# New ranks for a list-scheduled eight-layer kernel, and idle TensorE products on the input instead of the identity

## The chip, the cores and the metric

The kernel runs on one core of a Trainium2 chip. The core has five engines that each work through their own queue of instructions in order: TensorE (PE in the profile; its weight loads are PEld), VectorE (DVE), ScalarE (ACT), GpSimd (POOL) and SyncE (SP), which here only issues DMAs. The metric is the time of one execution on the device in microseconds. Runs of one kernel differ somewhat, so a median of several is given, with the lowest and the highest.

## The reference, cut to what matters

The input x has 8 sequences of 256 tokens with 128 channels, all float32. Eight layers follow each other, each as a residual on a layer norm of its input:

```python
x = x + causal_attention(layernorm(x))      # softmax over a lower triangle
x = x + ffn_relu(layernorm(x))              # 128 -> 512 -> 128, with a layer norm of its own at the end
x = x + linear_attention(layernorm(x))      # no softmax
x = x + ffn_relu(layernorm(x))
x = x + retention(layernorm(x))             # 16 heads, decay mask, head norm, silu gate
x = x + ffn_silu(layernorm(x))              # 128 -> 384 -> 128, integer weights scaled by 1/127
x = x + softmax_attention(layernorm(x))     # 16 heads of 8, with low-rank additions to the weights
x = x + ffn_silu(layernorm(x))
```

Within a layer the sequences are independent of each other.

## The kernel before, in words

The 8 sequences are taken in four groups of two, so a group is 512 tokens: four tiles of 128 tokens by 128 channels, kept in x[0] to x[3]. Each group goes through the eight layers in order; the last two are one function, softmax_attention_and_ffn. The four groups are independent, and their work is interleaved on the engines so that one group's products run while another's normalisations, copies and exponentials are under way. Everything goes through 8 PSUM banks, 28 "work" buffers and some smaller pools.

The order of the instructions is not written down. The class Plan is a list scheduler that runs in Python while the kernel is built. Every layer is a generator that yields steps such as "0.86 us on PE" or "give me a bank"; Plan keeps a model clock for each engine, picks for the engine that is free first the step that is able to start and has the smallest key, and lets that generator emit its instructions. The order in which it does so is the order in which they stand in each engine's queue on the chip. The key of a step is the rank of its thread, plus LATE if the step on PE has only just become able to start, and then its age. RANKS holds one rank for each group and layer (a lower rank goes first; the eighth number of a row is that of the last ffn_silu). FIRST and LAST are the ranks of the side jobs: FIRST for the causal weights and for the function pairs_of_scores, LAST for constants, linear_weights, retention_weights, silu_weights and softmax_weights. The last argument of plan.start is the model time before which a job doesn't start. LEEWAY is a model delay between the moment when a score bank has been read and the moment when it counts as free.

The lines that matter below, by the numbers that the profile uses:

- keep_busy (L379) issues products of the identity with itself into a bank that nobody reads. They stand six times at the very start, and four times behind the causal weights' products (L442, L443).
- layernorm: statistics of a tile on VectorE (L511, L512), the reciprocal root on VectorE or GpSimd (L518, L519) and GpSimd (L522, L523), and the scaling on ScalarE (L529) or VectorE (L534), whichever the plan finds free.
- transposed (L549): four transposes of a normalised tile on TensorE, and a copy out of PSUM (L414, on ScalarE or VectorE).
- causal_attention: L587 and L600 value and query products, L622 scores, L627 and L631 mask and maximum on VectorE, L634 exponentials on ScalarE, L641 transposes, L649 to L651 products with the values.
- ffn_relu: L719 (up) and L732 (down). linear_attention: L684 to L696. ffn_silu: L1045, L1051, L1061.
- retention: L855 are the score products (32 rows by 64 columns, 1024 matmuls in the profile), L913 the products within a chunk ("within", 64 by 32, 1024 matmuls), L890, L935 and L943 the rest; L840 masks the scores on VectorE.
- softmax attention: pairs_of_scores issues the score products (L1131) into score banks; VectorE finds maxima of them (L1152) for the first pass, which are transposed (L1165) and sent into l_spread by a DMA (L1173); ScalarE takes exponentials (L1186) in the second pass; L1203 are products with the values, L1216 transposes.
- constants: L430 and L434 fill r_values, l_values, r_spread and l_spread with zeros and ones on ScalarE, once. linear_weights has the product of L457, softmax_weights that of L491.

A float32 product is two passes: it appears in the profile as two weight loads and two matmuls. A transpose is one of each.

## Time and profile before

| | |
|---|---|
| median of 3 runs | 454.65 us (451.44, 454.65, 459.67) |
| the profiled execution | 459.54 us, its span 457.8 us, mean granted clock 0.981 |
| TensorE matmul busy | 436.2 us, 95% |
| VectorE busy | 338.9 us, 74% |
| ScalarE busy | 236.7 us, 52% |
| GpSimd busy | 132.3 us, 29% |
| DMA | 10.90 MB, 24 GB/s mean |

The span runs from the first to the last instruction of the program; the execution's own time has 1.7 us more around it. The profile is one execution, and it lies at the upper end of the runs. In the profile's slices the span is cut into 40 parts of 11.4 us; a digit is the busy share in tenths, PEclk the clock that TensorE was granted. A wait is given as what waited, what it waited for, the sum, how many times, and the longest. "issue" is a wait for which the profile shows no cause. A busy TensorE is not TensorE at its peak: matmuls are pipelined and their ends are modelled.

### The profile page before, as it was taken

The page shows a single profiled execution, that of the slowest core. Times are in us where ns is not written, and L with a number is a line of the kernel's source. Part 1 is how long each engine was busy: PE and PEld are TensorE (multiplying, and loading weights), DVE is VectorE, ACT ScalarE, POOL GpSimd, SP SyncE. Part 2 cuts the span into 40 slices and gives each one's busy share as a digit, 9 for nine tenths or more (in the row PEclk, how much of TensorE's full clock was granted, in tenths as well). Part 3 has the DMA queues.
Part 4 walks back from the last instruction along what each step waited for, and adds up shares of the span by engine and source line. Part 5 has one row for each costly group of instructions (what it writes and reads, how often), then busy time and mean ns, then how long its engine had stood idle before and what let it go on. Part 6 is the DMA issues. An engine that isn't in the chain of part 4 may idle for free.

```text
span 457.8 us, 13125 instructions
## 1 busy us (share of the span) xinstructions
PE 436.2 (95%) x5360; PEld 306.1 (67%) x5360; DVE 338.9 (74%) x979; ACT 236.7 (52%) x497; POOL 132.3 (29%) x239
## 2 busy tenths in 40 slices
PE   7999899999899999989989999989999999999987
PEld 6777687758667675764856556766676665656566
DVE  6698888898689789597958778957697652865143
ACT  3579844653532453413448363477844357264851
POOL 4145658776424541112221120230120021000120
PEclk9999899999999999995989999999999999999999
DMA  7300000003003002500001013000200001100001
GB/s 274 127 0 2 1 1 0 1 13 35 5 18 35 3 3 40 56 2 2 6 3 27 4 35 37 4 5 5 42 9 14 14 26 23 27 2 14 2 2 34
DMA packets 8044, 10.90 MB, mean 24 GB/s; under 512 B 1001, under 2 KB 6889, under 8 KB 7985
## 3 DMA queue, kind: packets, MB, share of 16 engines
q1 hardware_dynamic: 7904, 9.94, 10.0%
q8 instruction: 42, 0.69, 0.6%
q14 instruction: 18, 0.14, 0.1%
q10 hardware_dynamic: 80, 0.13, 0.1%
HBM read 4.56 MB, written 1.05 MB: 12 GB/s over the span
## 4 chain that ended last, share of the span: by engine, by line
PE 74%; DVE 12%; ACT 5%; issue 3%; POOL 2%; DMA 1%; SPq 1%; DVEq 0%
PE bank L1131 17%; PE bank L1203 7%; PE bank L1061 5%; PE bank L1045 5%; PE bank L1051 4%; PE bank L855 4%; PE bank L719 3%; PE bank L732 3%; PE bank L587 3%; PE bank L549 2%; PE bank L890 2%; PE bank L788 2%; PE bank L913 2%; DVE small L511 2%; DVE small L1152 2%
## 5 line engine op out<-in xcount | busy, mean ns | idle before, releaser
L1152 DVE TENSOR_REDUCE small<-bank 128x2 f32<-128x512 f32 x128 | 80.7, 683 | 28.3 <-PE bank L1131 28.1
L1186 ACT ACTIVATE probs<-bank 128x512 f32<-128x512 f32 x128 | 68.1, 598 | 53.0 <-PE bank L1131 50.6
L1131 PE MATMUL bank<-l_spread 32*128 32x256 f32 x1024 | 89.3, 409 | 2.3 <-issue 2.3
L1131 PEld LDWEIGHTS bank<-l_spread 32*128 32x128 f32 x1024 | 56.1, 188 | 26.3 <-issue 12.0
L518 POOL TENSOR_SCALAR small<-small 128x4 f32<-128x4 f32 (+1 forms) x40 | 10.0, 250 | 216.2 <-DVE small L512 201.2
L414 ACT COPY work<-bank 128x512 f32<-128x512 f32 (+3 forms) x86 | 40.2, 484 | 53.5 <-PE bank L549 14.3
L529 ACT ACTIVATE work<-x,small 128x128 f32<-128x128 f32 x80 | 34.7, 485 | 37.8 <-POOL small L523 37.6
L522 POOL TENSOR_TENSOR small<-small,mhalf 128x4 f32<-128x4 f32 (+1 forms) x45 | 43.8, 973 | 6.1 <-DVE small L519 6.1
L511 DVE BATCH_NORM_STATS2 small<-x 128x6 f32<-128x128 f32 x128 | 34.6, 271 | 3.7 <-DMA x<-in_x 3.2
L1203 PE MATMUL bank<-probs,l_values 128*32 128x256 f32 x512 | 34.0, 390 | 0.5 <-DVE work L1225 0.5
L512 DVE BATCH_NORM_AGGREGATE small<-small 128x2 f32<-128x6 f32 x160 | 29.1, 182 | 5.6
L732 PE MATMUL bank<-c_relu,work 128*128 128x128 f32 x256 | 31.9, 277 | 0.0
L719 PE MATMUL bank<-work,c_relu 128*128 128x512 f32 x64 | 30.9, 602 | 0.3 <-DVE work L414 0.3
L732 PEld LDWEIGHTS bank<-c_relu,work 128*128 128x128 f32 x256 | 30.2, 192 | 1.0 <-issue 0.7
L582 DVE TENSOR_TENSOR x<-bank,x 128x256 f32<-128x256 f32 (+1 forms) x36 | 15.9, 448 | 13.2 <-PE bank L587 4.2
L1045 PE MATMUL bank<-work,c_ints 128*128 128x256 f32 (+1 forms) x72 | 24.8, 462 | 0.5 <-ACT work L414 0.5
L1203 PEld LDWEIGHTS bank<-probs,l_values 128*32 128x32 f32 x512 | 13.9, 111 | 16.7 <-issue 6.1
L414 DVE COPY work<-bank 128x512 f32<-128x512 f32 (+3 forms) x26 | 13.7, 535 | 15.2 <-PE bank L1203 6.6
L549 PE MATMUL bank<-ident,work 128*128 128x128 f32 x128 | 23.8, 301 | 0.9 <-ACT work L529 0.7
L1061 PE MATMUL bank<-c_ints,work 128*128 128x128 f32 x192 | 24.6, 279 | 0.1
L1061 PEld LDWEIGHTS bank<-c_ints,work 128*128 128x128 f32 x192 | 22.9, 192 | 2.2 <-issue 1.0
L1051 PE MATMUL bank<-work,c_ints 128*128 128x256 f32 (+1 forms) x72 | 24.0, 456 | 0.0
(151 smaller groups left out, 784.8 us busy)
## 6 DMA issues: line engine op xcount, KB each, us to landing
r_spread<-wide SPq DMA_DIRECT2D x32, 64.0 KB
l_spread<-wide SPq DMA_DIRECT2D x32, 64.0 KB
out<-x SPq DMA_DIRECT2D x8, 128.0 KB
c_retention_qk<-in_retention_qk SPq DMA_DIRECT2D x1, 770.0 KB
x<-in_x SPq DMA_DIRECT2D x3, 256.0 KB
c_retention_vo<-in_retention_vo SPq DMA_DIRECT2D x1, 713.0 KB
c_relu<-in_relu SPq DMA_DIRECT2D x1, 706.0 KB
c_ints<-in_ints SPq DMA_DIRECT2D x1, 576.0 KB
```

The costliest lines, as they stand in the source:

```text
L414: (nc.scalar.copy if e == ACT else nc.vector.tensor_copy)(dst, src)
L511: nc.vector.bn_stats(stats[:, i, :], src[:, i, :])
L522: nc.gpsimd.tensor_tensor(rstd, rstd, minus_half[:, :nt], ALU.pow)
L719: nc.tensor.matmul(ps, w1[:, c * P : (c + 1) * P], yT[:, :N], start=True, stop=True)
L732: nc.tensor.matmul(ps[:, n * D : (n + 1) * D], h[c][:, i * P : (i + 1) * P], w2[:, c, :], start=(c == 0), stop=(c == 3),)
L1045: nc.tensor.matmul(ps[:, :n], w_gate[:, cols], yT[:, :n], start=True, stop=True)
L1051: nc.tensor.matmul(ps[:, :n], w_up[:, cols], yT[:, :n], start=True, stop=True)
L1061: nc.tensor.matmul(ps[:, (i - first) * D : (i - first + 1) * D], h[c][:, i * P : (i + 1) * P], w_down[:, c, :], start=(c == 0), stop=(c == 2),
L1131: nc.tensor.matmul(to[k][:, n * S : (n + 1) * S], seq.spread[rows, j, of_keys, n * P : (n + 1) * P], seq.spread[rows, j, 1 - of_keys, :], ...
L1152: nc.vector.tensor_reduce(nmax[:, h2 % 4 // 2, 2 * (h2 % 2) + k, :], ps[k].rearrange("p (m s) -> p m s", m=2), AX.X, ALU.max, negate=True,)
L1186: nc.scalar.activation(p[:, k, :], ps[k], AF.Exp)
L1203: nc.tensor.matmul(o[32 * i : 32 * (i + 1), (j % 2) * S : (j % 2 + 1) * S], seq.v[:, c, VONE * h : VONE * h + 32], seq.p[h2][0][:, k, c * ...
```

## The change

All 32 ranks, FIRST, LAST and LATE get new numbers, LEEWAY goes from 0.29 to 0.03, and the side jobs get new start times. These change no instruction of their own; they change the order in which Plan emits nearly all of them, and which of ScalarE and VectorE takes a copy or a scaling. The products of keep_busy take the first tile of the input x[0] in both places instead of the identity, and three of them stand at the start instead of six. The first causal attention of group 0 gets three more of them behind its transposes, into a bank of their own; the plan counts 0.21 us for each.

```diff
-LEEWAY = 0.29
+LEEWAY = 0.03
...
 RANKS = [
-    [-0.43, -1.33, -1.23, -2.16, 0.4, -1.26, 1.32, 4.87],
-    [-0.32, 1.61, 0.5, 1.51, -0.96, -0.46, -1.85, 1.67],
-    [2.33, 2.23, 2.97, 7.68, 2.15, -1.02, 3.92, 2.82],
-    [3.09, 3.56, 6.8, 10.82, 2.27, 3.76, -2.79, 2.52],
+    [-4.13, -2.77, -1.79, -1.45, 1.42, 1.01, -0.24, 3.83],
+    [-1.82, 0.93, 5.08, 2.15, 1.79, 4.87, 0.66, 0.66],
+    [-0.37, 1.61, -4.13, 2.32, 5.49, -4.05, 3.4, 4.38],
+    [3.42, 6.69, 6.1, 9.09, 1.61, 0.82, 1.3, 1.92],
 ]
-FIRST, LAST = -3.5, 11.78
-LATE = 1.95
+FIRST, LAST = -4.34, 9.59
+LATE = 1.56
...
-            nc.tensor.matmul(ps[:, :P], ident, ident, start=True, stop=True)
+            nc.tensor.matmul(ps[:, :P], x[0][:, 0, :], x[0][:, 0, :], start=True, stop=True)
 
-    keep_busy(banks[0], 6)
+    keep_busy(banks[0], 3)
...
-    def transposed(y):
+    def transposed(y, waiting=0):
 
         nt = y.shape[1]
         yT = yield get(work)
         ps = yield get(bank)
-        yield step(PE, 0.11 * nt)
+        idle = (yield get(bank)) if waiting else None
+        yield step(PE, 0.11 * nt + 0.21 * waiting)
         for i in range(nt):
             nc.tensor.transpose(ps[:, i * P : (i + 1) * P], y[:, i, :], ident)
+        if waiting:
+            keep_busy(idle, waiting)
+            put(bank, idle)
...
-        yT = yield from transposed(y4)
+        yT = yield from transposed(y4, 3 if parts == 2 else 0)
...
-    plan.start(constants(), LAST, 29.7)
-    plan.start(linear_weights(), LAST, 8.6)
-    plan.start(retention_weights(), LAST, 27.1)
-    plan.start(silu_weights(), LAST, 22)
-    plan.start(softmax_weights(), LAST, 57.7)
+    plan.start(constants(), LAST, 31.1)
+    plan.start(linear_weights(), LAST, 11.9)
+    plan.start(retention_weights(), LAST, 47.5)
+    plan.start(silu_weights(), LAST, 22.5)
+    plan.start(softmax_weights(), LAST, 19)
```

Here parts is 2 only in the causal attention of group 0.

## The prediction

> **What bounds the kernel now.** I read the page first: shares, slices, chain.

> ```profile
> PE 436.2 (95%) x5360; PEld 306.1 (67%) x5360; DVE 338.9 (74%) x979; ACT 236.7 (52%) x497; POOL 132.3 (29%) x239
> ...
> PE   7999899999899999989989999989999999999987
> ...
> PEclk9999899999999999995989999999999999999999
> ...
> PE 74%; DVE 12%; ACT 5%; issue 3%; POOL 2%; DMA 1%; SPq 1%; DVEq 0%
> ```

> TensorE is busy nearly throughout, but the chain is its own for 74% only, and its clock dips in three slices. Next the chain in order of time: where is it not TensorE's?

> ```profile
> 36.62 2.57 PE bank L732 x24
> 39.20 3.78 ACT r_spread L434 x4
> ...
> 46.99 2.82 ACT l_spread L434 x3
> 49.82 0.89 ACT work L634 x4
> 50.70 1.54 ACT work L529 x4
> ```

> From 39 to 53 us it runs through ScalarE, at 60 to 70 through VectorE's statistics (L511, L512). Up to about 160 us TensorE and its feeders share the bound; from there PE rows dominate. Then stretches, cut by me at the clock's steps (columns: length, busy of PE, PEld, DVE, ACT, POOL, clock, DMA share, GB/s):

> ```profile
> 50.10:53.50 3.40, 2.08 (x8) 0.96 (x8) 3.19 (x16) 3.40 (x14) 2.04 (x6) 1.00 0.00 0
> 53.50:56.90 3.40, 3.35 (x13) 2.79 (x14) 1.92 (x10) 2.25 (x6) 2.14 (x5) 0.50 0.01 2
> ...
> 203.70:207.10 3.40, 1.93 (x81) 1.58 (x71) 3.40 (x7) 1.54 (x4) 1.66 (x4) 1.00 0.00 0
> 207.10:210.50 3.40, 3.40 (x18) 1.72 (x10) 3.40 (x8) 0.69 (x2) 1.27 (x1) 0.50 0.01 2
> 210.50:214.00 3.50, 3.50 (x21) 1.96 (x20) 1.74 (x6) 1.39 (x2) 1.52 (x2) 0.50 0.02 5
> 214.00:217.40 3.40, 3.40 (x4) 0.94 (x4) 1.83 (x3) 0.98 (x2) 0.00 (x0) 0.51 0.00 0
> 227.60:231.00 3.40, 1.19 (x120) 1.21 (x98) 1.78 (x4) 1.75 (x4) 1.73 (x3) 1.00 0.02 5
> 231.00:234.40 3.40, 3.36 (x28) 2.08 (x31) 1.39 (x3) 1.08 (x2) 0.00 (x0) 0.50 0.02 5
> ```

> A stretch in which TensorE idles 1.3 to 2.2 of 3.4 us is followed by half clock: for one, three and one such stretches, five in all, each losing 1.7 us of work: 8.5 us. A cold start is hidden from the clock column; the durations of L600 show it (min/median/max ns):

> ```profile
> L600 PE MATMUL bank<-work,a_w x8: 592/595/1061, 12.9 to 31.1; 128*128 128x512 f32 x8
> ```

> 1061 ns at 13 us against 592 later. Last, TensorE's waits:

> ```profile
> PE bank L913 <- issue: 3.8, 2, 2.1
> PE bank L1131 <- issue: 2.3, 1, 2.3
> PE bank L457 <- DMA c_linear<-in_linear: 1.9, 1, 1.9
> PE bank L1165 <- DVE small L1152: 1.6, 2, 1.5
> ```

> The three "issue" waits end at 121.05, 231.04 and 306.40.

> [...] The three waits of about 2 us did not all trip it; only 231 did. [...] The trace has 42 packets and 0.69 MB on its instruction queue. I counted TensorE's instruction list (a float32 product is two loads and two matmuls, a transpose one of each, waits one): the three issue waits fall at counts 1985, 5569 and 7873, each a multiple of 256 less 63. So they are block boundaries. [...] here three cost 6.1 us.

> **The change, step by step.** The sum is made against the profiled execution, 459.54 us (span 457.8), the top of the runs shown; their median 454.65 is 4.9 us, or three half-clock windows, below it.

> 1. Start. Six identity products become three on the input; they must wait for x, which lands at 3.24 (VectorE's first row) instead of starting at 1.42. L442 still starts near 4.5 and the first transposes at 7.3, when VectorE and ScalarE deliver. Three more products (0.43 us each when cold) then fill 8.35 to 9.63, and the product of L457, which waited until 10.28 for its weights, stands behind group 1's transposes. L587 thus starts near 9.6 instead of 11.0: 1.4 us. If real data wake the clock one window sooner, another 1.9 follow: 3.3. Identity products ran from 1.4 to 7.5 without waking it, but no row shows input products. Yet the chain is ScalarE's and VectorE's by 39 us, so an earlier TensorE mostly waits longer. Bounds 0 and -3.3; I take -1.0.

> 2. Idle at 50 to 53.5, 1.86 us, plus one window, 1.7. It ends with the last exponentials L634. In the new order one spread copy of L434 (1.05 us) stands behind them; summing row durations ahead of the last exponential, ScalarE carries 33.2 us for 36.2 and VectorE 49.1 for 51.9. But VectorE's chain at 60 to 70 comes next. Bounds 0 and -3.6; I take -1.0. L491's products move forward by some 37 us of work and wait for the last load; the loads are over by 16 us (DMA share 0.01 from 16.0 to 22.9), so nothing queues behind them.

> 3. Idle at 204.6 to 206.1, 1.47, and its three windows, 5.1. Four maxima (L1152, 2.48 us together) stand between the scores and transpose L1165, covered by one block of L855 alone, 1.16. In the new order twelve products of L1061 stand there: 24 x 0.119 = 2.85, enough. This lies where TensorE is the bound: -6.6. If VectorE's backlog is longer, only the place changes; lower bound of the gain 0.

> 4. The window at 231: -1.7 (bounds 0, -1.7).

> 5. Instruction blocks. In the old order the three waiting blocks hold 1.5 us of work (L913 takes about 12 ns per matmul, 128 in a block) and waited 1.7 to 2.3: a block needs about 3.4 us. Adding row durations block by block and taking what is missing to 3.4 gives 7.1 us before (6.1 seen) and 9.7 after: pairs at blocks 8 and 9 (1.1 + 1.1), 14 and 15 (0.9 + 1.9), 20 (1.6) and 22 (0.4), 30 and 31 (1.8 + 0.8). Those before about 160 us may hide behind VectorE. Bounds +0.7 and +2.6; I take +1.5.

> 6. New half-clock windows at those places: between none and two each, 0 to +13.7; I take one, +1.7, since two of three such waits tripped nothing.

> 7. LEEWAY 0.29 to 0.03: a score bank is handed on 0.26 us earlier in the planner. With row durations laid along each order (queueing at the releasing engine left out), all score products but two before and three after have their bank free over 0.5 us ahead of use: I take 0; bounds 0 and 64 groups x 0.26 = +16.6, the upper end held by no row. The new tail puts 0.7 us of L1061 ahead of its last wait: -0.3 at best, 0 taken.

> Sum: 459.5 - 1.0 - 1.0 - 6.6 - 1.7 + 1.5 + 1.7 = 452.4. Run to run the number of windows varies, so I keep it against the median too: 454.65 holds about two windows, one remains (-1.7), idle 1.47 goes, starts give 2.0, blocks cost 1.5: 451.0. I forecast 451.6, midway.

> **The rivals.** *Everything counts* (chance 0.2): steps 1 and 2 keep their whole gain and no window runs cold: 459.5 - 3.3 - 3.6 - 6.6 - 1.7 + 0.7 = 445.0. For it: PE is busy 95%. Against: the chain at 39 to 70. *Only moved* (0.2): the early gains are absorbed, windows trip as often as in the median run, blocks cost their +1.5: 456. For it: the ranks remove no TensorE work; the product count is the same but for timing. *Crowded blocks* (0.1), the one that ends slower: the paired blocks idle TensorE 2.0 to 2.8 us within 4 us, as long as the 2.2 at 229 which halved the clock. Two windows at each of four places: 459.5 - 6.6 - 1.7 + 2.6 + 13.7 = 467.5. Without early gains it passes the median from one window on, and 463.7 from six.

> **How the numbers follow.** The likeliest case (0.5) gives 451.6, itself 448 to 455. A measurement here tells about 2% from no change: below 445.6 or above 463.7. Faster: half of the first rival and a little of the main case, 0.14; slower: most of the last, 0.08; same: 0.78. The range, from just under the first rival to short of the last: 445 to 460.

> **What would show it.** Right: L587 first near 9.6; L1165 no longer waiting 1.5 us; issue waits at more places than three, in L913; half-clock slices fewer than three. Step 1 is wrong if L600's maximum stays at 1061 ns or the early gain survives to 160 us. The whole is wrong if the issue waits go away or each trips the clock.

## The result, and the profile after

The changed kernel takes 452.68 us in the median of 20 runs (450.76 to 454.24); the kernel before, run beside it on the same chip, takes 456.15 (20 runs, 451.44 to 460.92). The ratio is 0.9942, with a 95% interval of 0.9921 to 0.9963: a small gain, inside the 2% that was forecast as "no change", and 1.1 us from the 451.6 forecast. The ratio leaves out executions that lie more than 1.5% above the fastest of their kernel, so it is nearer to one than the quotient of the medians (0.9924). The profiled execution took 452.34 us, its span 450.5, granted clock 0.991 (before: 459.54, 457.8, 0.981).

In the changed kernel all line numbers beyond the transposes are four higher: L600 has become L604, L913 L917, L1131 L1135, L1165 L1169; the transposes themselves are L550.

The page of the changed kernel, shares, slices of TensorE and of its clock, chain:

```profile
PE 427.5 (95%) x5360; PEld 300.0 (67%) x5360; DVE 345.9 (77%) x992; ACT 245.0 (54%) x492; POOL 133.5 (30%) x239
...
PE   7899899899999998999999999999999999999996
...
PEclk9999899999999998999999999999999999999999
...
PE 72%; DVE 18%; issue 4%; POOL 2%; ACT 2%; DMA 1%; SPq 0%; POOLq 0%; DVEq 0%; ACTq 0%
```

TensorE's busy time fell by 8.7 us although it computes the same: half-clock stretches count as busy (3.40 of 3.40 us from 207.10 on, before), and fewer are left (three windows of 3.4 us make up to 5.1 of it, and the cold start, now shorter, counts as busy too). Busy time is less than the sum of the matmuls, which overlap in the profile: the 1024 of L913, 225 ns each, make 12.9 us of it before. VectorE and ScalarE carry 7 and 8 us more; the plan deals out copies and scalings differently (979 instructions became 992, 497 became 492). The chain's share of ScalarE went from 5% to 2%, that of VectorE from 12% to 18%: the early bound has changed its engine. The chain in order of time (start, length, what) shows where. Before, it ran from 39 to 53 us through ScalarE's copies of L434; now it runs through VectorE, then one normalisation:

```profile
41.84 2.15 DVE work L534 x2
43.99 0.66 DVE work L728
...
46.57 0.52 DVE small L635 x2
47.09 0.60 DVE x L754
...
50.46 1.01 POOL small L522
```

Stretches of the changed kernel, cut at the steps of its clock; the last is the one in which TensorE had waited before (columns as in the prediction: start and end, length, busy of PE, PEld, DVE, ACT, POOL, clock, DMA share, GB/s):

```profile
49.97:53.38 3.41, 2.24 (x11) 1.24 (x12) 3.27 (x16) 3.33 (x9) 1.62 (x5) 1.00 0.01 2
53.38:56.79 3.41, 3.41 (x11) 2.38 (x11) 3.33 (x7) 1.76 (x4) 3.15 (x5) 0.50 0.00 0
169.43:172.84 3.41, 1.34 (x136) 1.18 (x119) 1.61 (x2) 0.59 (x1) 2.14 (x2) 1.00 0.02 5
172.84:176.26 3.42, 3.34 (x14) 1.44 (x14) 1.53 (x3) 0.58 (x1) 0.00 (x0) 0.50 0.00 0
203.70:207.10 3.40, 3.40 (x12) 1.37 (x14) 3.40 (x7) 1.79 (x3) 0.00 (x0) 1.00 0.00 0
```

Two half-clock windows (stretches of 3.4 us at half clock) where there were five. The one at 53 has stayed. The one at 172.84 is new and follows 2.1 us of idle. Between 203.7 and 207.1, where TensorE was idle for 1.47 us and then cold for three windows, it is now busy without a break. One profile does not show all places: in the ten profiles of the new order that this document draws on, a window begins at 52 to 54 us in four, at 90 to 91 in three and at 173 to 176 in eight. The one at 90 follows a wait of 1.82 us for ScalarE's copy L414, ahead of L700, that stands in all ten (the last of the waits below; the kernel before has none there). Among TensorE's waits (what, for what: sum, times, longest) L1169 is no longer near the top, and the waits of which the profile shows no cause lead the list:

```profile
PE bank L917 <- issue: 5.0, 6, 2.1
PE bank L379 <- DMA x<-in_x: 3.3, 1, 3.3
PE bank L700 <- ACT work L414: 1.8, 1, 1.8
```

The cold start no longer reaches the query products (the same line's durations as in the prediction, min/median/max ns):

```profile
L604 PE MATMUL bank<-work,a_w x8: 592/594/595, 10.6 to 33.3; 128*128 128x512 f32 x8
```

To see where the time went I laid the measured row durations along each order and took the difference between a product's start and its place in that sum. This is an estimate, since the places move by some tens of microseconds with the way the rows are weighed. Against the kernel before, the changed one is about 3.2 us ahead after 10 us of work, 1.0 behind after 80, 5.8 behind after 160 (its wait and window at 172 lie there, while the old order was still covered), 2.1 ahead after 210 (the gap of 206 and its windows), 4.4 ahead after 350 and 7.3 at the end.

### The profile page after: what moved, and what is told of

Read it like the earlier page. It is cut to its first block, busy times and chain, and to the rows that moved or that the text cites. A ratio compares the mean times of both kernels' runs of the same rounds, so it can differ in the third digit from the quotient of the medians.

```text
span 450.5 us, 13165 instructions
## 1 busy us (share of the span) xinstructions
PE 427.5 (95%) x5360; PEld 300.0 (67%) x5360; DVE 345.9 (77%) x992; ACT 245.0 (54%) x492; POOL 133.5 (30%) x239
## 3 DMA queue, kind: packets, MB, share of 16 engines
HBM read 4.56 MB, written 1.05 MB: 12 GB/s over the span
## 4 chain that ended last, share of the span: by engine, by line
PE 72%; DVE 18%; issue 4%; POOL 2%; ACT 2%; DMA 1%; SPq 0%; POOLq 0%; DVEq 0%; ACTq 0%
PE bank L1135 16%; PE bank L1207 7%; PE bank L1065 5%; PE bank L1049 5%; PE bank L859 4%; PE bank L736 4%; PE bank L1055 4%; PE bank L723 3%; DVE work L534 3%; DVE small L511 3%; PE bank L917 3%; DVE small L512 2%; PE bank L894 2%; PE bank L591 2%; PE bank L1220 2%
## 5 line engine op out<-in xcount | busy, mean ns | idle before, releaser
L1135 PE MATMUL bank<-l_spread 32*128 32x256 f32 x1024 | 86.5, 401 | 0.0
L518 POOL TENSOR_SCALAR small<-small 128x4 f32<-128x4 f32 (+1 forms) x40 | 11.8, 295 | 242.7 <-DVE small L512 227.2
L414 ACT COPY work<-bank 128x512 f32<-128x512 f32 (+3 forms) x77 | 37.1, 492 | 68.1 <-PE bank L550 27.2
L1135 PEld LDWEIGHTS bank<-l_spread 32*128 32x128 f32 x1024 | 54.5, 184 | 25.7 <-issue 11.3
L529 ACT ACTIVATE work<-x,small 128x128 f32<-128x128 f32 x70 | 30.6, 487 | 26.6 <-POOL small L523 26.5
L511 DVE BATCH_NORM_STATS2 small<-x 128x6 f32<-128x128 f32 x128 | 34.7, 271 | 3.9 <-DMA x<-in_x 3.5
L414 DVE COPY work<-bank 128x256 f32<-128x256 f32 (+3 forms) x35 | 17.9, 521 | 22.8 <-PE bank L1207 12.3
L1207 PE MATMUL bank<-probs,l_values 128*32 128x256 f32 x512 | 33.2, 384 | 1.1 <-DVE work L1057 0.6
L736 PE MATMUL bank<-c_relu,work 128*128 128x128 f32 x256 | 32.4, 278 | 1.2 <-DVE work L728 1.2
L736 PEld LDWEIGHTS bank<-c_relu,work 128*128 128x128 f32 x256 | 30.3, 192 | 4.7 <-issue 2.4
L512 DVE BATCH_NORM_AGGREGATE small<-small 128x2 f32<-128x6 f32 x160 | 29.1, 182 | 5.5
L723 PE MATMUL bank<-work,c_relu 128*128 128x512 f32 x64 | 32.2, 618 | 0.1
L726 ACT ACTIVATE work<-bank,c_relu 128x512 f32<-128x512 f32 x26 | 17.9, 687 | 16.7 <-PE bank L723 15.7
L1049 PE MATMUL bank<-work,c_ints 128*128 128x256 f32 (+1 forms) x72 | 25.3, 463 | 0.7 <-ACT work L414 0.7
L1065 PE MATMUL bank<-c_ints,work 128*128 128x128 f32 x192 | 24.6, 279 | 0.5 <-ACT work L414 0.5
L1051 ACT ACTIVATE work<-bank 128x256 f32<-128x256 f32 (+1 forms) x36 | 15.7, 454 | 16.7 <-PE bank L1049 16.4
L1065 PEld LDWEIGHTS bank<-c_ints,work 128*128 128x128 f32 x192 | 22.9, 192 | 2.7 <-issue 1.1
L1055 PE MATMUL bank<-work,c_ints 128*128 128x256 f32 (+1 forms) x72 | 24.6, 458 | 0.0
```

Of the source, the lines that this page charges most:

```text
L414: (nc.scalar.copy if e == ACT else nc.vector.tensor_copy)(dst, src)
L511: nc.vector.bn_stats(stats[:, i, :], src[:, i, :])
L723: nc.tensor.matmul(ps, w1[:, c * P : (c + 1) * P], yT[:, :N], start=True, stop=True)
L736: nc.tensor.matmul(ps[:, n * D : (n + 1) * D], h[c][:, i * P : (i + 1) * P], w2[:, c, :], start=(c == 0), stop=(c == 3),)
L1049: nc.tensor.matmul(ps[:, :n], w_gate[:, cols], yT[:, :n], start=True, stop=True)
L1055: nc.tensor.matmul(ps[:, :n], w_up[:, cols], yT[:, :n], start=True, stop=True)
```

## The experiments

**Which part does it: the idle products or the order?** Four kernels on one chip, beside 70 runs of the kernel before (457.0 us). The first gives the kernel before the input in its idle products and leaves everything else:

```diff
 # before
-            nc.tensor.matmul(ps[:, :P], ident, ident, start=True, stop=True)
+            nc.tensor.matmul(ps[:, :P], x[0][:, 0, :], x[0][:, 0, :], start=True, stop=True)
```

> The kernel before with x[0] in place of the identity in the ten idle products at the start, order unchanged. Theory (feeders absorb an early TensorE): the clock wakes one or two 3.4 us windows sooner, so the longest L600 falls from 1061 ns towards 592, but VectorE and ScalarE set the pace to about 160 us of the span and the time stays within 0.5 us of before. Rival (idle products carry the gain): about 1.5 to 3 us faster than before. Second rival (data does not matter): L600 stays near 1061 ns and the time at before.

Measured: 457.76 us, ratio 1.0042 (1.0013 to 1.0071). The clock rose at 15.10 us, and the maximum of L600 stayed at 1061 ns, as the second rival had it. The input in place of the identity gains nothing; if anything it costs 0.4%.

The second also moves three of the six products behind the first transposes, as the change does, in the old order:

```diff
 # before, with the edit above
-    keep_busy(banks[0], 6)
+    keep_busy(banks[0], 3)
...
-    def transposed(y):
+    def transposed(y, waiting=0):
...
+        if waiting:
+            keep_busy(banks[1], waiting)
...
-        yT = yield from transposed(y4)
+        yT = yield from transposed(y4, 3 if parts == 2 else 0)
```

> The kernel before with all of the idle products of the change (three on x at the start, four, and three behind the first transposes of group 0, written to a bank that the next products overwrite), old order otherwise. Theory: clock awake near 9 to 12.6 us instead of 16, gain under 1 us at the end of the run (ratio 0.998 to 1.000). Rival (idle products carry the gain): ratio near 0.994, as the whole change.

Measured: 454.78 us, ratio 0.999 (0.9962 to 1.0018). The clock rose at 14.81 us all the same, so the expected 9 to 12.6 was a miss. Its median lies 2.2 us under the kernel before; resampling the 22 and 70 runs gives -3.5 to +0.3 for that difference, so it isn't settled.

The third is the change without any of the idle products' edits: six of the identity at the start, none behind the transposes, new order. (The plan still sets aside their bank and their 0.21 us each, so that the order stays the same.)

```diff
 # changed
-            nc.tensor.matmul(ps[:, :P], x[0][:, 0, :], x[0][:, 0, :], start=True, stop=True)
+            nc.tensor.matmul(ps[:, :P], ident, ident, start=True, stop=True)
...
-    keep_busy(banks[0], 3)
+    keep_busy(banks[0], 6)
...
-            keep_busy(idle, waiting)
```

> The changed kernel's order with the old idle products: six and four on the identity, none behind the first transposes. Theory: the gain lies after 190 us of the span and comes from the order, so the time is that of the changed kernel within 1 us (452.7, ratio 0.992 to 0.996). Rival (idle products carry the gain): at the time of before, 456.

Measured: 452.94 us, ratio 0.9915 (0.9892 to 0.9937): all of the gain. The fourth is the changed kernel with the identity in its idle products (the first hunk above alone):

> The changed kernel with the identity back in its ten idle products, same places. Theory: L604 at 10.6 us of the span takes about 1061 ns per matmul again because the clock wakes at 12.6 or 16 instead of 9, and the time is within 1 us of the changed kernel. Second rival (data does not matter, being busy does): clock awake at 9 as in the changed kernel.

Measured: 452.86 us, ratio 0.9929 (0.9905 to 0.9953). The expectation that the clock then rises only at 12.6 or 16 us was a miss: it rose at 8.03, and in the third kernel at 4.58, when six identity products and the beginning of the causal weights' were all that had run. So products of the identity can wake the clock, and when it wakes makes no difference to the time here. What follows: **the order is the change**. In the new order the idle products add nothing that these runs show (452.94 us without their edits, 452.86 with the identity in all of them); whether they gain something in the old order is the open 2.2 us above.

**Are the waits in L917 the edges of instruction blocks?** A block is put here at 256 instructions of TensorE's list, since the waits stand multiples of 256 apart (1985, 5569 and 7873 in the prediction). The page has 42 packets and 0.69 MB on the instruction queue, 16.4 KB each; TensorE's list has 10,825 instructions in the trace of the kernel before, 258 to a packet. In the traces of both kernels the closest two of these packets start 3.41 us apart (before; 3.45 in the changed kernel), and each of the nine waits over 0.3 us for which no cause is shown ends 1.27 to 1.49 us after one of them has landed. Sixteen tiny products ahead of everything move every block edge by 64 instructions; the order of all else is unchanged.

```diff
 # changed
+    for _ in range(16):
+        nc.tensor.matmul(banks[0][:32, :8], ident[:, :32], ident[:, :8], start=True, stop=True)
     keep_busy(banks[0], 3)
```

> The changed kernel with sixteen tiny products (32 columns by 8 of the identity) put ahead of everything, while TensorE waits for x anyway: 64 more instructions at the head of TensorE's list, the order of all else unchanged. Block theory: the places where TensorE waits for instructions are multiples of 256 in its list, so they fall on other work. Row durations block by block, 3.4 us needed for each: the computed stalls go from 9.7 to 5.4 us. The waits near 218.7 and 226.3 us of the changed kernel and the first one near 298 vanish, the wait of 2.15 near 173 becomes shorter (1.9 at most), and the sum of waits without a shown cause goes from 5.0 to about 3. Time 1 to 3 us below the changed kernel, about 450.5. Rival (the waits belong to the work that stands there, such as the bursts of tiny products, and not to the count): the same waits at the same places and sizes, sum 5.0 again, time 452.7.

Its waits:

```profile
PE bank L919 <- issue: 4.2, 3, 1.9
...
PE bank L861 <- issue: 0.4, 1, 0.4
```

The waits against those computed from row durations, with the prediction's estimate of 3.4 us needed for a block of 256 (us; place in the span):

| changed kernel | computed | measured | shifted by 64 | computed | measured |
|---|---|---|---|---|---|
| 122.0 | 1.07 | 0.49 | 117.9 | 0.95 | 0.38 |
| 125.5 | 1.10 | 0.80 | 125.3 | 1.10 | 1.10 |
| 172.9 | 0.87 + 1.93 | 2.15 | 172.4 | 1.93 | 1.88 |
| 218.7 | 1.63 | 0.43 | - | none | none |
| 226.3 | 0.36 | 0.43 | - | none | none |
| 298.7 | 1.75 + 0.83 | 0.74 | 298.4 | 0.83 | 1.24 |
| all, with those under 0.4 | 9.7 | 5.0 | | 5.3 | 4.6 |

The waits go with the count and not with the work: those at 218.7 and 226.3 are gone, though the same products stand there. Counted in TensorE's list of weight loads, matmuls and waits, those of the changed kernel come after 1985, 2241, 3777, 5057, 5570 and 7873 instructions, those of the shifted one after 1729, 2241, 3777 and 7873: each is a multiple of 256 and 193 more, to within one. So is every wait of this kind over 0.3 us in all fourteen profiles of this document. So the block edges are shown. Their size was computed too large where the shortfall is small or where two short blocks follow each other. The time was 451.83 us (6 runs). Against all 42 runs of the changed kernel, taken in two other rounds, that is 0.9976 (0.9944 to 0.9991 by resampling), 1.1 us, at the low end of the 1 to 3 expected; the sum of waits was to be 3 and is 4.6, a miss.

**Does the gap at 206 cost what step 3 says?** First taken away from the kernel before, by six products in front of the transpose that waited:

```diff
 # before
+        if seq.g == 0 and seq.b == 0 and half == 1:
+            for _ in range(6):
+                nc.tensor.matmul(ps[:, :P], w_lora_o, w_lora_o, start=True, stop=True)
         nc.tensor.transpose(ps[:16, :P], flat_nmax, ident)
...
+            seq.b = b
```

> The kernel before with six products of a constant put right ahead of the one transpose L1165 that waited 1.47 us for VectorE at 206 us, into the bank that the transpose then overwrites; the order is otherwise unchanged. Theory (step 3: the idle stretch halves the clock for up to three windows): the idle there falls from 1.47 to under 0.5 and no half-clock slice follows at 207; the median falls by 1.5 to 3.5 us, since the windows strike in part of the executions only, to about 453.5. Rival (the idle stretch costs only itself, or the windows come elsewhere): the six products cover an idle that VectorE would have caused anyway, no gain, 457. If they come late, the products themselves cost up to 1.4 us.

Measured: 455.39 us against 457.94 beside it, ratio 0.998 (0.9944 to 1.0017). The wait of 1.47 is gone and no window follows at 207, but the interval of the ratio holds both no gain and 2.5 us: inconclusive.

Then added to the changed kernel at a clean place. GpSimd, which is empty there, holds back the fifth L1169 by multiplications by one:

```diff
 # changed; 14 in one kernel, 20 in the other
+        todo["turned"] = todo.get("turned", 0) + 1
+        for _ in range(14 if todo["turned"] == 5 else 0):
+            nc.gpsimd.tensor_scalar(flat_nmax, flat_nmax, 1.0, None, ALU.mult)
         nc.tensor.transpose(ps[:16, :P], flat_nmax, ident)
```

> The changed kernel with fourteen multiplications by one on GpSimd (0.23 to 0.31 us each, on an engine that is empty there from 265 to 280 us) put between the maxima and the fifth transpose L1169, which in the changed kernel starts at 272.99, 2.4 us after the last maximum. TensorE then waits there for 0.9 to 2.0 us, about as long as the stretch of 1.47 us that step 3 priced at 6.6 with three half-clock windows; its order is unchanged, and no profile so far shows a window within 40 us of the place. The runs of the changed kernel had 1.4 half-clock windows on average, those of the kernel before 3.4, each worth 1.2 us by their slope. Theory (an idle stretch of that length halves the clock in a part of the executions, for one window): windows rise to 1.7 to 2.1 on average, the median by 1.5 + 0.6 = 2 us, to about 455. Step 3 as it was priced (three windows each time): 4 or more windows, 458. Rival (it costs only itself or nothing): windows stay at 1.4, 453 to 454.4.

> The same with twenty multiplications: TensorE waits there for 2.3 to 3.9 us. Theory: one window nearly always follows, so 2.2 to 2.5 windows on average and 453 + 3.0 + 1.2 = 457. Step 3 as it was priced: three windows, 460. Rival (windows have nothing to do with this wait): 1.4 windows, 455 to 456.

The multiplications took 0.33 us each, start to start, so the waits came out longer than expected: 2.3 us in place of 0.9 to 2.0, and 4.3 in place of 2.3 to 3.9. With fourteen, the wait, the 3.4 us up to the clock's step, in which it lies, and the 3.4 us after:

```profile
PE bank L1172 <- POOL small L1171: 2.3, 1, 2.3
```

```profile
272.24:275.65 3.41, 1.11 (x18) 0.71 (x11) 2.48 (x4) 0.36 (x2) 2.13 (x9) 1.00 0.00 0
275.65:279.06 3.41, 3.41 (x7) 1.35 (x6) 0.55 (x2) 0.60 (x1) 0.00 (x0) 0.50 0.01 2
```

With twenty, the clock falls while TensorE still waits:

```profile
272.30:275.71 3.41, 0.44 (x9) 0.04 (x4) 2.48 (x4) 0.00 (x0) 2.53 (x11) 1.00 0.00 0
275.71:282.54 6.83, 5.50 (x11) 2.72 (x11) 1.24 (x3) 0.85 (x2) 1.01 (x4) 0.50 0.00 1
```

A wait of 2.3 us brings one half-clock window, one of 4.3 us brings two. Every run lists its mean granted clock, and a window of 3.4 us in some 450 lowers it by 0.0038 (half of 3.4/450), so windows can be counted, to the nearest whole one, in runs without a profile. The last column is the line through each kernel's own runs: its time at no window, and what one more window adds. The slopes are good to about 0.2 (before) and 0.5 (changed), the times at no window to 0.5 and 0.7; the changed kernel's runs have one or two windows only, so its 451.5 lies outside them.

| kernel | runs | median us | windows, mean | us at none + us per window |
|---|---|---|---|---|
| before (four rounds) | 146 | 456.64 | 3.23 | 453.1 + 1.16 |
| changed (two rounds) | 42 | 452.90 | 1.36 | 451.5 + 1.13 |
| changed, wait of 2.3 | 22 | 456.39 | 2.32 | |
| changed, wait of 4.3 | 6 | 459.89 | 3.17 | |

The ratios to the kernel before are 1.002 (1.0 to 1.004) and 1.0102 (1.0054 to 1.0151). The 2.3 us wait adds 3.5 us (452.90 to 456.39) and 0.96 windows: itself and one window. The 4.3 us wait adds 7.0 and 1.8 windows: itself and 2.7. These two kernels and the changed one ran in different rounds; their ratios to the kernel before beside them, set against 0.9942 and 0.9952 for the changed kernel, say the same (3.1 to 3.6 us and 6.9 to 7.3 us more). The theory's medians, 455 and 457, were too low; its waits were shorter than the ones that came out. The rival, that windows have nothing to do with it, falls; so does "three windows each time", for waits of these lengths. A wait of 1.47 us was not added anywhere.

**Why does one wait halve the clock and the next not?** Within each profile, the clock's steps lie whole multiples of 3.413 us apart (in the changed kernel at 9.01, 53.38, 56.79, 172.84 and 176.26: 13, 1, 34 and 1). So within an execution there is a fixed grid of 3.413 us, and where it falls differs from one to the next: after the start of the span, the first edge lies at 2.2 us in the changed kernel, and in the two runs below at 2.8 and 0.1. Cut along this grid, the traces of two runs give a likely reason for a pair that looks alike. The shifted kernel waited 1.88 us at 172.4, within one stretch; with pairing and shift together (below) it waited 1.86 us at 172.0, of which an edge at 170.72 cut off 0.6. First the shifted kernel, then the other, each with the stretch after:

```profile
170.07:173.49 3.42, 1.54 (x85) 1.03 (x68) 1.43 (x3) 1.07 (x2) 1.57 (x1) 1.00 0.00 0
173.49:176.90 3.41, 3.41 (x25) 2.08 (x25) 1.76 (x3) 0.40 (x3) 0.00 (x0) 0.50 0.02 5
...
170.72:174.13 3.41, 2.13 (x46) 1.18 (x46) 1.13 (x3) 0.59 (x1) 0.53 (x1) 1.00 0.02 5
174.13:177.54 3.41, 3.41 (x72) 3.13 (x70) 2.00 (x6) 2.06 (x6) 0.00 (x0) 1.00 0.00 0
```

Over all fourteen profiles, up to 440 us, nine stretches at full clock have TensorE busy for at most 1.34 us, and half clock follows all nine; it follows 16 of the 44 with 1.50 to 2.26 us, and one of the 1688 with more. What decides in the middle group is not shown, nor why half clock lasted three windows after 206 us in the kernel before, with TensorE busy throughout.

**Do lone pairs of score products cost as much as two?** A group of L1135 normally scores two pairs of heads, but near the end some score one. The chain of the changed kernel there:

```profile
380.06 1.06 PE bank L1135 x8
381.12 1.00 PE bank L1207 x16
382.12 1.08 PE bank L1135 x16
```

Eight matmuls hold the path for 1.06 us, sixteen for 1.08. The prediction had no such term. In the trace of the changed kernel 20 of its 74 groups are lone pairs (19 by themselves, as the expectations count them, and one right beside a group of two), in that of the kernel before 22 of 75. The edit lets a second pair join a little earlier:

```diff
 # changed
-                    if sum(i[0] <= plan.now for i in score_bank.items) > 1:
+                    if sum(i[0] <= plan.now + 0.2 for i in score_bank.items) > 1:
```

> The changed kernel with one threshold in pairs_of_scores moved: once only softmax attention is left, a group of score products takes a second pair of heads along when the banks come free within 0.2 us of the model, not only when they are free already. The order is unchanged up to product 2640 of 2828 (about 390 us); behind it 17 groups of a lone pair remain in place of 19, and 54 of two pairs in place of 53. Theory (a lone pair of heads holds TensorE 1.07 us, nearly as long as two pairs with 1.12): 2 x 1.07 - 1.12 = 1.0 us less, 451.6. Rival (the lone groups lie beside waits for banks that the pairing only moves): no difference, 452.7; if pairs then wait for banks, up to 0.5 us slower.

Measured: 451.89 us (9 runs), against the 42 runs of the changed kernel 0.9978 (0.9962 to 0.9994), 1.0 us less, as computed, though the two were not run side by side. So the changed kernel was run again, beside one with this edit and the shift by 64 together:

> The changed kernel once more, unchanged, as the neighbour of the two runs below on the same chip: 452.7 us, 0.99 to 0.996 of the kernel before.

> The changed kernel with both small edits at once: sixteen tiny products at the head (64 more instructions on TensorE's list) and pairs taken along when banks come free within 0.2 us. Theory (the two gains lie in different stretches, waits for instructions at 218 to 298 us and lone pairs after 390 us, and TensorE is the bound in both): 0.8 + 1.0 below the unchanged one beside it, about 451. Rival (each of them was the difference between two chips or two days): within 0.3 us of the unchanged one.

Measured on that chip: 453.35 us for the changed kernel (22 runs, 0.9952 of the kernel before, 0.9932 to 0.9972), 449.75 for both edits (6 runs, 448.57 to 451.81; 0.9898 of the kernel before, 0.9845 to 0.9951). Between the two the ratio of medians is 0.9921 (0.9901 to 0.9951 by resampling): 3.6 us less (2.2 to 4.5), more than the 1.8 expected; where the rest comes from is open. Its windows are 1.17 on average against 1.41, which at 1.2 us each is 0.3 us of it, and its line, through six runs, stands at 448.6 with none. Its profile has no window at all, although the wait at 172 is there with 1.86 us, cut by the grid as above. On this chip this version beats both kernels.

**Is LEEWAY worth nothing?**

```diff
 # changed
-LEEWAY = 0.03
+LEEWAY = 0.29
```

> The changed kernel with LEEWAY back at 0.29, all ranks and start times as in the change; every decision of the plan behind the first score products may come out differently. Step 7's view (LEEWAY moves only banks that are free long before use): 452 to 453 us. Rival (LEEWAY decides, through the test whether banks are free at that moment, how many score groups run with a lone pair, and the ranks fit one LEEWAY only): 25 lone groups stand in the order in place of 19 and the planner's own clock ends 17 us later, so 465 to 470 us, with TensorE idle in new places.

Measured: 471.05 us, ratio to the kernel before 1.0318 (1.0241 to 1.0396), 17.7 us above the changed kernel beside it. 26 lone groups stand in place of 20 (25 and 19 by themselves). From the start of each score product to that of the next instruction on TensorE, the products of L1135 take 92.9 us in place of 81.7, 3.5 of it in waits; that is most of the 13.0 us between the two profiled spans. Why groups of two pairs take longer there was not tried. With the new ranks the old LEEWAY makes a bad plan. This doesn't say what the change's 0.26 us is worth, because the old ranks were made for the old value.

## Why the prediction was right, and where its steps were not

The number was right within 1.1 us and the mechanism of most of the gain was the one named: fewer stretches in which TensorE idles, and so fewer half-clock windows. By the table the gain between all runs of both kernels, 456.64 to 452.90, is 3.7 us: 1.87 windows fewer at 1.16 us make 2.2, and the time at no window fell by 1.6. The forecast was set midway between a sum for one profile (452.4) and one for the median (451.0). By steps:

1. **Start**, -1.0. L591 starts at 9.65, as computed (9.6). The clock rose at 9.01, so the early gain came near the whole bound, 3.2 of 3.3 us, and it was gone by 80 us, absorbed as argued, with VectorE on the chain there; the third kernel, without the edits of the idle products, kept all of the gain. What failed is the reason given: that the input might wake the clock where the identity does not. Why the clock rose at 4.6 to 12 us in every profile of the new order, and at 14.8 to 16.0 in three of four of the old one, is open; the products ahead of it differ too little. In the fourth of the old one it rose at 4.54 and fell again at 11.36, after a wait of 2.47 us for L457's weights.
2. **Idle at 50**, -1.0. Wrong: the stretch before that window still has 1.17 us of idle (1.32 before; the 1.86 of the prediction also counts waits outside it), and the window came. The chain moved from ScalarE to VectorE; the order was still ahead there (L736 starts at 62.08, L732 at 63.40 before), but the lead was gone near 95 us of the span, after the wait of 1.82 us before L700. No step had that wait, nor that it brings a window in three profiles of ten. By the curve the new order is then behind until about 190 us: the sum of the first two steps was -2.0, and the curve shows +5.8 at 160.
3. **Idle at 206**, -6.6. The idle went as the order said: twelve products of L1065 stand ahead of that transpose, now at 214.93, and it starts without a gap. The size was that of one execution: three windows at 1.7 us. The same wait of 1.47 us stands in two more profiles of the old order, with one window after it in one and none in the other, where an edge of the grid cuts it. The added waits show one window for 2.3 us, and the runs put one window at 1.1 to 1.2 us; that it is less than 1.7 because part of it falls where TensorE isn't the bound is likely, but not shown. For the median the price is, as an estimate, 1.5 and up to 1.2.
4. **Window at 231**: gone, worth about 1.2 us by the slope rather than 1.7. The prediction noted that only one of the three waits of about 2 us tripped the clock: along the grid, TensorE was busy for 1.19 us of the 3.41 there, for 1.71 and 1.61 at the other two.
5. **Instruction blocks**, +1.5. Right places, shown by the shift; wrong sizes. 5.0 us (6.1 in a second profile) in place of 9.7, against 6.1 before: the term is about 0 or -1, not +1.5.
6. **New windows**, +1.7 for one. Right: the window at 172.84 follows the longest of those waits. One begins there, between 172.8 and 175.9 us, in eight of the ten profiles of the new order; by the slope it cost 1.2 us rather than 1.7.
7. **LEEWAY and tail**, 0. Mis-sized in the tail: 2.9 of the curve's 7.3 us come between 350 and 380 us of work. There a wait of 0.81 us at L1216 is gone, and 22 groups of a lone pair became 20, with 54 of two pairs in place of 53: 2 x 1.07 - 1.12 = 1.0 us. The other 1.1 us has no account. The bound of the prediction counted 64 groups; there are 75 before and 74 after. LEEWAY as a term of its own says little: the same 0.26 us, put on the new ranks, costs 18 us.

The errors offset each other: steps 1 to 3 promised too much, steps 5 and 7 too little. That is the luck in the number. Of the rivals, "everything counts" failed, for the early lead was lost, near 95 us of the span rather than between 40 and 75; "only moved" is right for the first 190 us alone; "crowded blocks" failed, for the paired waits at 122 and 125 us (0.5 and 0.8) were followed by no half clock, and one place in four tripped. Stretches of the grid with 1.11 us of TensorE work in them (the added wait of 2.3) and with 1.54 (the shifted kernel) were followed by half clock. At block edges, 3.6 to 6.4 us of waits stand open in each of the ten profiles of the new order.

## What to carry to other kernels

Count half-clock windows over many runs from the mean granted clock before pricing one profile's windows: one window here is 1.2 us, an idle TensorE stretch of 2.3 us costs itself and one window, and the same program can show five windows in one execution and none in another (the kernel before, at mean granted clocks of 0.981 and 0.999). To see whether a wait is at risk, lay the 3.413 us grid through the steps of the profile's clock. Where tiny products fill an instruction list, find the waits without a cause and see whether they stand a multiple of 256 instructions apart, as here; 64 instructions at the head moved them here. In a list-scheduled kernel look for operations that cost the same half full and full (here a lone pair of score products), and test the planner's constants only together with its ranks.
